# Row factors brought to the partitions by DMA instead of by a selection matmul, in the last attention and the last experts of an eight-layer kernel

## The chip, the cores and the metric

The kernel runs on one core of a Trainium2 chip. A core has five engines, each with its own instruction stream worked off in order: TensorE (PE in the profile, with its weight loads as PEld), VectorE (DVE), ScalarE (ACT), GpSimd (POOL) and SyncE (SP). They hand work to each other through semaphores. Transfers are issued by an engine's instruction stream (here SP, ScalarE or GpSimd) and carried out by 16 DMA engines that all share. An instruction that waits holds up all that stands behind it on its engine. The metric is the device time of one launch in microseconds, on the slowest core; with one core there is no other.

## The reference

Four batches of 512 rows with 128 features each pass through eight layers, attention and feed-forward in turn, each followed by an added residual and a layer norm. Two layers matter here.

The last attention has 16 heads of 64 and clipped relative positions, for keys and for values:

```
sim  = q k^T * scale + q . rel_k_table[idx] * scale
attn = softmax(sim)
out  = attn v + attn . rel_v_table[idx]
y    = out Wo^T + bo
```

The last layer is a mixture of 16 routed experts of width 64 (four of them chosen for each row, out of two of four groups) and a shared expert:

```
weights, idx = gate(x)                       # per row, 4 of 16 experts
combine = sum over the 4 of one_hot(idx) * weights
routed  = einsum(silu(x w1_e) * (x w3_e), w2_e, combine)
shared  = (silu(x w1_s) * (x w3_s)) w2_s
```

Both layers need one number per row and head (1 over the softmax sum) or per row and expert (the combine weight), multiplied on data that lie with heads or experts on the partitions and rows along the free dimension.

## The kernel before

The layers are stages that run one after another; what a stage leaves over at its end runs beside the next one's start. Inside a stage, work is written as generators ("a slot" is one step of all that are live), and a scheduler orders the instructions of each engine from that.

**Third attention (class `A3`).** (In the kernel's naming; it is layer 3 counted from 0.) Work is cut into 32 units of two heads: unit `t` is pair `t % 8` of batch `t // 8`. Eight items (four blocks of 128 queries, two heads) make a unit, so a unit has eight slots. For each item `score` makes two products into a PSUM bank `s` (L1344, L1345), DVE adds a window and takes the row minimum (L1347, L1349), and ScalarE takes the exponential with the row sum into `den` (L1350). Two items later (`la = 2`) `turn` transposes the result `p` four times on PE (L219) and ScalarE copies it to `PT` (L1363); DVE sums the right part (L1368), and every second time SP stores a band of `p` to DRAM (`a3dpw`, L1372). At the end of a unit SP loads the band's diagonals back (`at`, L1376). `tail` then makes 16 value products in one run (L1393, "the value block"), which needs all `PT` of the unit, and later two small products from `at` (L1406, L1407); ScalarE copies the result to `OT` (L1409). `prep` makes the operands of the next unit: a ScalarE cast `H` (L1307), a DVE remainder `L` (L1308) and nine or so copies inside SBUF, nearly all on SP's queue (L1312). `half` makes, once for four units, the values `V` and the window data `bd`.

Four units make a half of a batch. After each half, `fin` (L1414) divides by the softmax sums. It takes the reciprocal `rd`, splits it in a high and a low part `lr` (L1423, L1424), transposes it to 16 rows, which ScalarE copies to `lT` (L1430), and then, for each of the four `OT` of the half, spreads two of these rows over 64 partitions each with a product by a 0/1 matrix `a3sel`, and multiplies:

```
nc.tensor.matmul(ps, w["sel"][:, pr, :], lT, start=True, stop=True)   # L1436
nc.vector.tensor_tensor(OT, OT, ps, ALU.mult)                          # L1437
```

Then the output product follows (L1447), and after the second half the layer norm. `fin` of the half that ends with unit `t - 1` starts in the first slot of unit `t + 1`, that is, one unit after `t - 1` is through its scores, because its last `OT` comes late in unit `t`.

PSUM: `s` has three banks, `t` two, `o` one and `b` two. Bank `b` serves `prep`, `half` and `fin` in turn.

**Last experts (class `F3`).** For each batch, `hidden` makes nine blocks of 128 hidden features (the shared one first, then eight pairs of experts), each from six products into two banks `s`. `gate` computes the combine weights of a batch on DVE and POOL, transposes them and has ScalarE copy them to `cT`. Four positions behind `hidden`, `weigh` spreads two experts' weights over the partitions with the same kind of product (L2287, bank `t`, of which there is one) and multiplies them on (L2288); two positions later `out` makes the products with the second weights (L2297). The gate of batch `c` is started `ahead = 7` positions before the batch's first `hidden`; a batch has nine positions. If the weights are not there when `weigh` needs them, it steps the gate until they are.

DMAs issued by SP and by ScalarE signal on a shared set of eight completion counters, taken in turn; each DMA waits until the one before it on its counter has landed.

Of the kernel before, what the change touches and what calls it, by code (L numbers as in the profile page):

```python
# [16 lines left out]
P = 128  # L17
NB = 4
# [21 lines left out]
class K:  # L40
# [249 lines left out]
    def split_w(self, pool, src, n, name, scales=(), tag=None, raw=("wraw", 1)):  # L290
# [5 lines left out]
        def fill():  # L296
            for s in range(0, n, 512):
# [10 lines left out]
                yield  # L308
        return h, l, fill()

    def mm3(self, out, wh, wl, xh, xl):
# [801 lines left out]
def a3_constants():  # L1113
    c = {}
    ql = np.arange(P)[:, None]
    x = np.arange(512)[None, :]
    c["c_right"] = (x >= ql).astype(np.float32)
    st = np.zeros((32, 2, 2, T), np.float32)
    for bk in range(32):
        st[bk, :, :, 16 * bk + 32:] = 1.0  # L1120
    c["c_step"] = st.reshape(64, 2, T)
    r = np.arange(16)[None, :]
    c["c_d16"] = (r < 16 - ql % 16).astype(np.float32)
    c["c_sel3"] = heads(8)
    return c


class A3:
# [93 lines left out]
    def operands(self):  # L1222
        k, nc, d, pool, w = self.k, self.nc, self.k.d, self.pool, self.w
        w["right"] = pool.tile([P, 512], BF16, name="a3right")
        nc.gpsimd.dma_start(w["right"], d["c_right"])
        w["sel"] = self.more.tile([P, 4, P], F32R, name="a3sel")
        self.lT = k.rows16(self.more, "a3lT")
        nc.gpsimd.dma_start(w["sel"], d["c_sel3"])

# [148 lines left out]
    def tail(self, t):  # L1378
# [33 lines left out]
        yield  # L1412

    def fin(self, b, hf, X):  # L1414

        k, nc, w, pool = self.k, self.nc, self.w, self.pool
        u = k.next()
        den = self.S[b][2]
        wait = k.turn if b == NB - 1 and hf else lambda: ()
        lr = self.more.tile([P, 4, 16], F32R, tag="lr", name=f"lr{u}", bufs=1)  # L1420
        rd = self.more.tile([P, 4, 8], F32, tag="rd", name=f"rd{u}", bufs=2)
        nc.vector.reciprocal(rd, den[:, :, 8 * hf:8 * hf + 8])
        nc.vector.tensor_copy(lr[:, :, 0:8], rd)  # L1423
        nc.vector.tensor_tensor(lr[:, :, 8:16], rd, lr[:, :, 0:8].bitcast(F32), ALU.subtract)  # L1424
        yield from wait()
        ps = k.bank("b")
        for c in range(4):
            k.tr(ps[:16, c * P:(c + 1) * P], lr[:, c, :])
        lT = self.lT
        nc.scalar.copy(lT[:16], ps[:16, :])  # L1430
        yield
        for pr in range(4):
            yield from wait()
            ps = k.bank("b")
            OT = self.S["O", b, 4 * hf + pr]
            nc.tensor.matmul(ps, w["sel"][:, pr, :], lT, start=True, stop=True)  # L1436
            nc.vector.tensor_tensor(OT, OT, ps, ALU.mult)  # L1437
            yield
# [20 lines left out]
    def run(self, Xs):  # L1459
# [5 lines left out]
        for t in range(n + 1):  # L1465
            if t + 1 < n:
                gs.insert(0, self.prep(t + 1))
            if 1 <= t <= n:
                gs.append(self.tail(t - 1))
            if t >= 5 and t % 4 == 1:  # L1470
                b, hf = divmod((t - 5) // 4, 2)
                gs.append(self.fin(b, hf, Xs[b]))
            if t % 4 == 1 and (t + 3) // 4 < 2 * NB:
                gs.append(self.half(*divmod((t + 3) // 4, 2), Xs[(t + 3) // 8]))
            for j in range(8):
                next(main, None)
                k.step(gs)
                if t > n // 2:
# [701 lines left out]
class F3:  # L2180


    nm, span, keep = "f3", None, True
    lag, ahead, steps = 4, 7, 2
    banks = dict(s=4, t=1, o=1, b=2)
# [17 lines left out]
    def gate(self, b, X):  # L2203
# [48 lines left out]
        nc.vector.reciprocal(den, den)  # L2252
        nc.vector.tensor_tensor(cw, cw, den[:, :, None].to_broadcast([P, 4, 16]), ALU.mult)

        c2 = pool.tile([P, 4, 32], F32R, tag="c2", name=f"c2{u}", bufs=2)
# [7 lines left out]
        yield  # L2263
        cT = self.cTs[b % 2]
        nc.scalar.copy(cT[:32], ps[:32, :])
# [16 lines left out]
    def weigh(self, b, j, h):  # L2282
        k, nc, w = self.k, self.nc, self.w
        while b not in self.cT:
            k.step(self.gs)
        cb = k.bank("t")
        nc.tensor.matmul(cb, w["sel"][:, j, :], self.cT[b], start=True, stop=True)  # L2287
# [20 lines left out]
    def run(self, Xs):  # L2308
# [14 lines left out]
        for i in range(9 * NB + self.lag + 2):  # L2323
            b, j = divmod(i, 9)
            j = (j + 8) % 9
            for c in range(1, NB):
                if i == max(9 * c - self.ahead, 0):
                    gs.append(self.gate(c, Xs[c]))
# [79 lines left out]
```

## Time and profile before

| | us |
|---|---|
| median of three runs | 2243.53 (2236.81 to 2244.39) |
| profiled execution | 2239.62, its span 2237.9 |
| third attention | about 1548 to 2105 of the span |
| last experts | about 2105 to 2237 |
| PE busy | 2025.4 (91% of the span) |
| DVE busy | 1664.1 (74%) |
| ACT busy | 1333.5 (60%) |
| POOL busy | 501.9 (22%) |
| mean granted TensorE clock | 0.965 |

The page lists the busy time of each engine first, then the span in 40 slices of about 56 us, in which a digit is the busy share in tenths. A "group" line names a source line, an engine, an operation and its tiles, how often it ran, its busy time and mean, and how long the engine stood idle just before it and for whom. A "wait" line reads: who waited, at which line, for whom, then total time, number and longest. The "chain" is the work that ended last, followed back from the end: it shows what really took the time where several engines are busy at once. Issuing a DMA and waiting count as no busy time; the queue lines (SPq, ACTq) show issues. Matmuls overlap each other, so the mean of a matmul in a group is longer than what it adds to the chain.

### The profile page before, as it was taken

To read this page: it belongs to the slowest core of one execution; us is meant where nothing else is said; L and a number is where in the kernel's file an instruction comes from. 1 tells how busy PE (TensorE), PEld (TensorE's weight loads), DVE (VectorE), ACT (ScalarE), POOL (GpSimd) and SP (SyncE) were. 2 spreads that over 40 slices of the span, in tenths; PEclk is the share of its full clock that TensorE was granted. 3 is DMA by queue.
4 is the path that set the end of the run, shared out by engine and by line. 5 is a ranking of instruction groups with operands and counts; after the bars stand their busy time and mean duration, and the time that the engine had idled before them with its cause. 6 is when DMAs were issued, how large, how long until landed. Compare 5 with 4: busy or idle time off the path is not lost.

```text
span 2237.9 us, 43122 instructions
## 1 busy us (share of the span) xinstructions
PE 2025.4 (91%) x14400; PEld 1477.7 (66%) x14400; DVE 1664.1 (74%) x5592; ACT 1333.5 (60%) x2983; POOL 501.9 (22%) x706
## 2 busy tenths in 40 slices
PE   7999788888888999999999999998999999999897
PEld 4666566676665667676887665786666566666676
DVE  5778689888878677873777785544777877778787
ACT  3566787787734656665333666333777777767632
POOL 3222212111212532433000322531111111111220
PEclk9999999999978999999999999999999999999999
DMA  5321322021433454421021420604888878888400
GB/s 171 106 77 35 109 50 57 6 48 27 116 113 108 130 175 125 127 65 57 15 67 48 116 78 15 219 17 112 214 209 198 211 192 193 199 194 211 99 5 15
DMA packets 264918, 242.10 MB, mean 108 GB/s; under 512 B 106352, under 2 KB 190618, under 8 KB 263866
## 3 DMA queue, kind: packets, MB, share of 16 engines
q1 hardware_dynamic: 259146, 221.33, 37.2%
q0 software_dynamic: 5232, 17.50, 3.3%
q8 instruction: 115, 1.88, 0.3%
q14 instruction: 105, 0.86, 0.1%
q10 hardware_dynamic: 320, 0.52, 0.1%
HBM read 103.82 MB, written 74.32 MB: 80 GB/s over the span
## 4 chain that ended last, share of the span: by engine, by line
PE 59%; DVE 17%; ACT 10%; DMA 7%; issue 4%; POOL 2%; SPq 1%; ACTq 0%; POOLq 0%; DVEq 0%
PE t L219 5%; PE s L2129 4%; PE o L1393 3%; PE o L744 3%; PE s L695 3%; PE t L728 3%; PE o L1032 3%; PE b L313 3%; PE b L219 3%; PE o L2025 3%; DMA a3dpw<-p 2%; PE s L313 2%; PE b L315 2%; PE b L314 2%; PE s L315 2%
## 5 line engine op out<-in xcount | busy, mean ns | idle before, releaser
L985 DVE CUSTOM_DVE_ANT_0 junk<-w,a1mask 128x640 bf16<-128x640 f32 x256 | 203.1, 818 | 67.3 <-PE w L983 65.4
L219 PE MATMUL t<-ident,p 128*128 128x128 f32 x1280 | 201.9, 279 | 23.8 <-ACT p L1350 15.7
L772 ACT ACTIVATE Pt<-t 128x384 f32<-128x384 f32 (+1 forms) x384 | 179.5, 528 | 65.8 <-PE t L728 54.4
L219 PEld LDWEIGHTS t<-ident,p 128*128 128x128 f32 x1280 | 151.7, 142 | 81.0 <-ACT p L1350 39.0
L1363 ACT COPY PT<-t 128x512 f32<-128x512 f32 x256 | 149.9, 596 | 71.9 <-PE t L219 70.9
L1059 ACT ACTIVATE Pt<-t 128x512 f32<-128x512 f32 x256 | 149.1, 597 | 72.7 <-PE t L1058 44.5
L1350 ACT ACTIVATE p<-s,nb 128x512 f32<-128x512 f32 x256 | 178.6, 702 | 12.8 <-DVE nb L1349 8.4
L1349 DVE TENSOR_REDUCE nb<-s 128x1 f32<-128x512 f32 x256 | 175.0, 687 | 2.6
L1368 DVE CUSTOM_DVE_ANT_0 jk<-p,a3right 128x496 bf16<-128x496 f32 (+3 forms) x256 | 125.0, 488 | 29.2 <-ACT p L1350 17.8
L697 DVE CUSTOM_DVE_ANT_0 junk<-s,a0mask 128x128 bf16<-128x128 f32 (+3 forms) x256 | 114.2, 485 | 43.4 <-PE s L695 42.4
L697 DVE CUSTOM_DVE_ANT_0 junk<-s,a2mask 128x128 bf16<-128x128 f32 (+3 forms) x256 | 114.9, 484 | 28.3 <-PE s L695 27.9
L781 POOL TENSOR_SCALAR_AFFINE_SELECT Pt<-Pt 128x512 f32<-128x512 f32 x112 | 69.9, 636 | 249.0 <-ACT Pt L772 248.9
L1344 PE MATMUL s<-a3KT,a3QT 128*128 128x512 f32 x256 | 118.9, 465 | 7.3 <-DMA a3K<-L 4.1
L1347 DVE TENSOR_TENSOR s<-s,W 128x160 f32<-128x160 f32 (+1 forms) x256 | 81.1, 318 | 56.1 <-PE s L1345 55.2
L1393 PE MATMUL o<-PT,V 128*64 128x512 f32 x512 | 116.9, 599 | 0.5 <-ACT PT L1363 0.5
L1707 ACT ACTIVATE p<-sm,nb 128x128 f32<-128x128 f32 x256 | 100.6, 396 | 24.8 <-DVE nb L1705 24.3
L1345 PE MATMUL s<-a3K,a3Q 128*128 128x512 f32 x256 | 102.7, 401 | 0.1
L1705 DVE CUSTOM_DVE_ANT_0 sm<-s,band,rn 128x128 f32<-128x128 f32 x256 | 78.3, 344 | 26.5 <-PE s L1692 19.3
L1056 PE MATMUL t<-a1Q,a1K 128*128 128x512 f32 (+3 forms) x256 | 92.4, 366 | 6.2 <-ACT Pt L1059 3.6
L695 PE MATMUL s<-a0K,a0Q 128*128 128x256 f32 (+2 forms) x256 | 83.6, 387 | 14.0 <-DVE mx L697 6.8
L982 PE MATMUL w<-a1K,a1Q 128*128 128x256 f32 (+2 forms) x192 | 83.8, 437 | 9.3 <-DVE mx L985 8.3
L2012 ACT ACTIVATE sl<-s 128x512 f32<-128x512 f32 x64 | 38.0, 598 | 91.0 <-PE s L315 85.6
(494 smaller groups left out, 5812.7 us busy)
## 6 DMA issues: line engine op xcount, KB each, us to landing
W<-a3dsk SPq DMA_DIRECT2D x32, 640.0 KB
a1Q<-a1iq SPq DMA_DIRECT2D x32, 512.0 KB
a3dpw<-p SPq DMA_DIRECT2D x64, 160.0 KB
a3dpw<-p SPq DMA_DIRECT2D x64, 144.0 KB
a1K<-a1ik SPq DMA_DIRECT2D x64, 128.0 KB
a3Q<-a3dim SPq DMA_DIRECT2D x32, 256.0 KB
a3KT<-H POOLq DMA_DIRECT2D x64, 128.0 KB, 4.4
a3KT<-H SPq DMA_DIRECT2D x64, 128.0 KB
```

Of the source, the lines that this page charges most:

```text
L219: return self.nc.tensor.matmul(out.bitcast(x.dtype), x, i[:n, :n], is_transpose=True, start=start, stop=stop)
L695: self.scored = nc.tensor.matmul(s[:, :nm], self.qof(0, t, i)[:, qc * P:(qc + 1) * P], Ks[:, i, :nm], start=True, stop=True).ins
L697: nc.vector.tensor_tensor_reduce(junk[:, :n], s[:, :n], k.mask[:, 512 - n:512], 1.0, NEG, ALU.add, ALU.max, mx[:, qc, i:i + 1])
L772: ready = nc.scalar.activation(Pt[:, i, z:], s[:, z:], AF.Exp, scale=sc).ins
L985: nc.vector.tensor_tensor_reduce(junk, s.rearrange("p a n -> p (a n)")[:, T - n:T + m], k.mask[:, T - n:T + m], 1.0, NEG, ALU.add, ALU.max ...
L1059: nc.scalar.activation(Pt[:, i, :T], s, AF.Exp, scale=sc)
L1344: nc.tensor.matmul(s, QT[:, e, qs], KT[:, e, :], start=True, stop=False)
L1349: nc.vector.tensor_reduce(nb, s, AX.X, ALU.min)
L1350: nc.scalar.activation(p[:, e, :], s, AF.Exp, bias=nb, scale=-1.0, accum_out=den[:, qc, 2 * un + e:2 * un + e + 1])
L1363: self.copied[t] = nc.scalar.copy(PT[e][:, :, qc * P:qc * P + P], tb.rearrange("p (c n) -> p c n", n=P)).ins
L1368: nc.vector.tensor_tensor_reduce(jk[:, :nn], p[:, e, x0:], w["right"][:, :nn], 1.0, 0.0, ALU.mult, ALU.add, at[:, e, qc, 31:32])
L1393: m = nc.tensor.matmul(o[64 * e:64 * e + 64, :], V[:, kc, h * 64:h * 64 + 64], PT[e][:, kc, :], start=(kc == 0), stop=False)
```

## The change

Both places get their spread rows from DRAM instead of from a product.

In the third attention a new generator `sums` starts one unit earlier than `fin` used to compute these numbers. It transposes the four columns blocks of the reciprocals as they are (f32, without the split), ScalarE copies eight rows, and ScalarE's own queue stores them to a DRAM tile and loads each row back to 64 partitions, two loads for each of four tiles `rb`. The first tile takes the space of a tile that was used in the setup, the third that of another stage's tile, the second and fourth share the two buffers of `rb` with the rows themselves. `fin` now waits three slots and only multiplies, on SBUF data. `a3sel` and its load, `lT` and its memset are gone.

In the last experts the same is done for the third and fourth batch (`b > 1`), on SP's queue: one store of 16 rows, then four loads of four rows to 64 partitions each. Their gates start nine positions ahead instead of seven. The first two batches keep the product.

```diff
+    def rows_out(self, rows, name, eng):
+
+        d = self.dr.tile([rows.shape[0], T], F32, tag=f"rows{rows.shape[0]}", name=name, bufs=2)
+        eng.dma_start(d, rows)
+        return d
+
+    def rows_in(self, dst, d, i, eng):
+
+        n = dst.shape[1] if len(dst.shape) > 2 else 1
+        for e in range(2):
+            ap = [[0, 64], [2 * T, n], [1, T]] if n > 1 else [[0, 64], [1, T]]
+            eng.dma_start(dst[64 * e:64 * e + 64], bass.AP(tensor=d.tensor, offset=d.offset + (i + e) * T, ap=ap))
...
 class A3: operands
-        w["sel"] = self.more.tile([P, 4, P], F32R, name="a3sel")
-        self.lT = k.rows16(self.more, "a3lT")
-        nc.gpsimd.dma_start(w["sel"], d["c_sel3"])
...
+    def sums(self, b, hf):
+
+        k, nc = self.k, self.nc
+        u = k.next()
+        rd = self.more.tile([P, 4, 8], F32, tag="rd", name=f"rd{u}", bufs=2)
+        nc.vector.reciprocal(rd, self.S[b][2][:, :, 8 * hf:8 * hf + 8])
+        yield
+        if b == NB - 1 and hf:
+            yield from k.turn()
+        ps = k.bank("b")
+        for c in range(4):
+            k.tr(ps[:8, c * P:(c + 1) * P], rd[:, c, :])
+        yield
+        lr = self.more.tile([P, T], F32, tag="rb", name=f"lrow{u}", bufs=2)[:8]
+        nc.scalar.copy(lr, ps[:8, :])
+        yield
+        rb = self.S["R", b, hf] = [pool.tile([P, T], F32, tag=tag, name=f"rb{u}{i}", bufs=n) for i, (pool, tag, n) in
+                                   enumerate(((self.early, "a3z", 1), (self.more, "rb", 2), (k.sh, "oT", 1), (self.more, "rb", 2)))]
+        rows = k.rows_out(lr, f"a3rows{u}", nc.scalar)
+        for i in range(4):
+            for _ in range(1 if i % 2 else 2):
+                yield
+            k.rows_in(rb[i], rows, 2 * i, nc.scalar)
+
     def fin(self, b, hf, X):
 
         k, nc, w, pool = self.k, self.nc, self.w, self.pool
         u = k.next()
-        den = self.S[b][2]
         wait = k.turn if b == NB - 1 and hf else lambda: ()
-        lr = self.more.tile([P, 4, 16], F32R, tag="lr", name=f"lr{u}", bufs=1)
-        rd = self.more.tile([P, 4, 8], F32, tag="rd", name=f"rd{u}", bufs=2)
-        nc.vector.reciprocal(rd, den[:, :, 8 * hf:8 * hf + 8])
-        nc.vector.tensor_copy(lr[:, :, 0:8], rd)
-        nc.vector.tensor_tensor(lr[:, :, 8:16], rd, lr[:, :, 0:8].bitcast(F32), ALU.subtract)
-        yield from wait()
-        ps = k.bank("b")
-        for c in range(4):
-            k.tr(ps[:16, c * P:(c + 1) * P], lr[:, c, :])
-        lT = self.lT
-        nc.scalar.copy(lT[:16], ps[:16, :])
-        yield
+        for _ in range(3):
+            yield
         for pr in range(4):
-            yield from wait()
-            ps = k.bank("b")
             OT = self.S["O", b, 4 * hf + pr]
-            nc.tensor.matmul(ps, w["sel"][:, pr, :], lT, start=True, stop=True)
-            nc.vector.tensor_tensor(OT, OT, ps, ALU.mult)
+            nc.vector.tensor_tensor(OT, OT, self.S["R", b, hf][pr], ALU.mult)
             yield
...
 class A3: run
+            if t >= 4 and t % 4 == 0:
+                sums = self.sums(*divmod((t - 4) // 4, 2))
             if t >= 5 and t % 4 == 1:
                 b, hf = divmod((t - 5) // 4, 2)
                 gs.append(self.fin(b, hf, Xs[b]))
...
             for j in range(8):
                 next(main, None)
+                if j == (self.la if t < n else 0) and t >= 4 and t % 4 == 0:
+                    gs.append(sums)
                 k.step(gs)
...
 class F3
-    lag, ahead, steps = 4, 7, 2
+    lag, ahead, steps = 4, 9, 2
...
 class F3: gate
+        if b > 1:
+
+            yield
+            yield from k.turn()
+            ps = k.bank()
+            for c in range(4):
+                k.tr(ps[:16, c * P:(c + 1) * P], cw[:, c, :])
+            yield
+            cr = pool.tile([16, T], F32, tag="cr", name=f"cr{u}", bufs=2)
+            nc.scalar.copy(cr, ps[:16, :])
+            cb = [pool.tile([P, 4, T], F32, tag="cb", name=f"cb{u}{i}", bufs=2) for i in range(2)]
+            rows = k.rows_out(cr, f"f3rows{b}", nc.sync)
+            for i in range(2):
+                k.rows_in(cb[i], rows, 8 * i, nc.sync)
+            self.cT[b] = cb
+            return
...
 class F3: weigh
+        if b > 1:
+            nc.vector.tensor_tensor(h, h, self.cT[b][j // 4][:, j % 4, :], ALU.mult)
+            return
...
 class F3: run
-                if i == max(9 * c - self.ahead, 0):
+                if i == max(9 * c - (self.ahead if c > 1 else 7), 0):
                     gs.append(self.gate(c, Xs[c]))
```

## The prediction

> **What bounds the kernel now.** I read the page first (shares and slices), then the stretches, the groups and the waits of the third attention, and last its time line and its chain.
>
> ```profile
> PE 2025.4 (91%) x14400; PEld 1477.7 (66%) x14400; DVE 1664.1 (74%) x5592; ACT 1333.5 (60%) x2983; POOL 501.9 (22%) x706
> ...
> PE   7999788888888999999999999998999999999897
> ```
>
> One core, TensorE busy nearly throughout. The change touches only 1620 to 2238 us: up to the first half of the third attention the instructions of both builds stand in the same order on every engine.
>
> ```profile
> 1700.00:1800.00 100.00, 93.92 (x537) 62.82 (x536) 78.58 (x231) 71.34 (x170) 13.61 (x23) 1.00 0.85 195
> 1800.00:1900.00 100.00, 92.68 (x507) 62.49 (x506) 77.82 (x229) 73.44 (x172) 13.35 (x23) 0.98 0.84 194
> ...
> 2150.00:2237.00 87.00, 73.58 (x447) 61.48 (x445) 71.22 (x246) 21.92 (x34) 15.42 (x20) 0.98 0.05 13
> ```
>
> The columns are the stretch, its length, busy time of PE, weight load, DVE, ACT and POOL, the clock, and the DMA engines' share. In the attention PE is busy 93%, ACT only 71 to 73%, but the 16 DMA engines 84%. In the experts (last line) PE and DVE are close together and DMA is empty. The next question is where ACT's missing quarter lies.
>
> ```profile
> L1350 ACT ACTIVATE p<-s,nb 128x512 f32<-128x512 f32 x242 | 168.8, 702 | 11.8 <-DVE nb L1349 8.0 <-ACT p L1350 1.1 <-ACT PT L1363 0.7
> ...
> L1436 PE MATMUL b<-a3lT,a3sel 128*128 128x512 f32 x28 | 13.0, 463 | 0.3 <-DVE OT L1437 0.3
> ```
>
> ```profile
> ACT PT L1363 <- PE t L219: 69.1, 67, 4.3
> ACT V L1280 <- PE b L315: 15.4, 14, 4.0
> ```
>
> Over half of ACT's waiting is 69.1 us for transposes, and the time line says when: while PE runs the 16 value products of one unit in a block (3.58 us), ACT runs dry; outside it ACT has little left.
>
> ```profile
> 1776.07 1.12 ACT L1363 COPY PT<-t 128x512 f32<-128x512 f32 x2
> 1777.03 0.75 ACT L1350 ACTIVATE p<-s,nb 128x512 f32<-128x512 f32 x1
> ...
> 1779.41 0.28 ACT L1350 ACTIVATION_READ_ACCUMULATOR p<-s,nb 128x1 f32 x1
> 1781.44 0.58 ACT L1363 COPY PT<-t 128x512 f32<-128x512 f32 x1 [1.75 <-PE t L219]
> 1783.34 0.59 ACT L1363 COPY PT<-t 128x512 f32<-128x512 f32 x1 [1.32 <-PE t L219]
> ```
>
> ```profile
> 1776.90 3.58 PE o L1393 x16
> 1780.49 0.43 PE b L1436
> 1780.91 0.44 PE t L219 x4
> 1781.35 0.23 PE b L1436
> ```
>
> From 1766.2 to 1779.7 ACT has one gap of 0.41 us. The block starts at 1776.90, right after the last PT copies; it needs them. So on the path PE and ACT alternate, and ACT work ahead of a block delays the block. The chain prices a sel product at 0.23 us, not the 463 ns of its group.
>
> **Part 1, third attention: what goes.** Per half of a batch (8 halves; in 7 the new work lies inside the loop): four products of `a3lT` with `a3sel`, 4 x 0.23 = 0.92 us of PE, and four turns of a PSUM bank `b`; on DVE the cast and the subtract of `lr`, 0.18 + 0.18 us. Each half takes some 24 banks `b`; waits of its weight loads and products for DVE's `L` are 13.4 + 9.2 us over the stage, so four banks fewer could give up to 4/24 x 22.6 = 3.8 us in all. POOL loses one load and one memset at the start, on no path.
>
> **What stays.** Four small transposes, now plain f32 (278 ns against 252 in the groups of L219): nothing to 0.1 us. The reciprocal and the ScalarE copy (570 ns) only move a unit earlier. The four multiplications read SBUF instead of PSUM. The nearest row for that form is
>
> ```profile
> L1669 DVE TENSOR_TENSOR kr<-kr,rn 128x512 f32<-128x512 f32 x32 | 21.2, 682 | 0.1
> ```
>
> against 680 ns for L1437: no gain. [...]
>
> **What comes.** Nine DMA issues per half on ScalarE's own queue: one store of 8 rows and eight loads of 64 x 2 KB. The trace has ScalarE issuing 64-partition DMAs only at the stage's start:
>
> ```profile
> 1546.50 0.62 ACTq L1312 DMA_DIRECT2D a3QT<-L  x1
> 1547.16 0.61 ACTq L1312 DMA_DIRECT2D a3Q<-H  x1
> ```
>
> That is 8 x 0.61 + about 0.4 (SP's `at` issue is 0.36) = 5.3 us of ACT per half, and it isn't in the busy sums. An issue may run beside the instruction before it; for the second of a pair nothing is left to hide under. In the changed order of instructions the first pair of loads stands ahead of the last two PT copies of the unit, so ahead of the block; the other three pairs stand after them, mixed with the exponentials, PT copies and `bd` copies of the next unit. Behind each waiting issue all of these queue, and PE waits for them.
> - Store and first pair: 0.4 + 1.2 us where ACT is full. From 0 (wholly beside other work) to 1.6; I take 1.5, since ACT has no gap there.
> - Three pairs: 3.7 us, against ACT's gaps from 1781.44 to 1795.30: 1.32 + 0.40 + 0.28 + 0.36 + 0.29 + 0.31 + 0.32 = 3.28 us.
> - Waits at the issue. The order shows that SP's and ScalarE's DMAs share eight completion counters in turn: each waits for the DMA eight before it. For ScalarE these are SP's `a3Q`, `at` and `a3KT` copies, or its own load of a pair before. The one landing that the trace prices for a 128 KB copy is POOL's a3KT, 4.4 us; its own load of 2.9 us earlier (two issues, an exponential, a copy) would cost 1.5 us. From 0 to a landing for each of three pairs, 13 us; I take 1.5, the nearest pair.
> So after the block 3.7 + 1.5 - 3.3 = 1.9 us, and per half 1.5 + 1.9 = 3.4. As ACT sets the pace there, PE's 0.92 us buys nothing. Seven halves: +24 us. I reduce it to +20, as DVE's short work and the fewer banks give some back.
>
> **DMA and SP.** 64 loads of 128 KB in all, 8 MB on 107. At the boundary of halves the DMA engines are least full (0.69 of 1777 to 1795), so I cost the traffic at nothing; if that room is not there, one landing, 4.4 us, per half. SP's DMAs wait for the shared counters of ScalarE's late loads: 0 to 4.4 us per half, taken as hidden by the same room. The last half lies beside the experts' start, where DVE splits weights: 0 to 4.4 us, taken as 0.
>
> [...]
>
> **Part 2, last experts, batches 3 and 4.**
>
> ```profile
> L2288 DVE TENSOR_TENSOR h<-h,t 128x512 f32<-128x512 f32 x32 | 21.8, 683 | 6.8 <-PE t L2287 6.3
> ```
>
> Sixteen sel products go: 16 x 0.23 = 3.7 us of PE, plus at most half of the 6.3 us that DVE waits for them. The multiplications cost the same. The gate starts two of nine positions earlier, 2 x 29/9 = 6.4 us (29 us is a third of the 87 us stretch). It must cover a store, then two 512 KB loads: f3sel, 512 KB on an empty queue, landed in 3.8 us, so some 2 + 3.8 + 1.9 = 7.7 us. Before, copy to first weighing was 2.1 us (2139.8 to 2141.9), so 8.5 us are there. SP has only output stores besides, and the second pair's wait for the buffers of batch 3 ends long before its use. I take -3 us; from -7 (all waits gone) to +8 (a landing uncovered in both batches).
>
> **Sum.** +20 - 3 = +17 us. The profiled execution took 2239.6 us (span 2237.9 and 1.7 around it), 3.9 under the median of the three runs. 2239.6 + 17 = 2256.6; half of that offset added, as a new median need not share it, gives 2258.5.
>
> **Rivals.** (a) The issues hide: ACT is idle 27% on average, and half of each pair may run beside an ACT instruction. Then PE's gain counts: 8 x 0.92 + 3.8 + 3 = 14 us, 2239.6 - 14 = 2226. Against it: ACT's idle time sits in the blocks, not where the issues stand. This is the case on the other side; it decides if ScalarE's holding time per half stays under the 3.3 us of gaps. (b) Waiting replaces issuing: the counters and the loads land late in 84% full DMA engines, ScalarE stands for one more 4.4 us landing per half: 7 x 4.4 = 31 us more, 2289. For it: SP already waits 53.3 us for `a3dpw` stores between 1600 and 2060. (c) The halves cancel: the first pair hides, 7 x 1.9 - 3 = +10, less 3.8 for banks: +6, 2246. That the change does not do what it says I exclude: the order shows both parts.
>
> **How the numbers follow.** Forecast 0.53 (own range 2250 to 2275), (a) 0.18, (b) 0.13, (c) 0.16. The range reaches to most of (a) and (b): 2229 to 2287. About 0.5%, 11 us, can be told from no change: against 2243.5, faster is below 2232 and slower above 2255. Faster 0.18; same: (c) and the lower edge of the forecast, 0.25; slower 0.57.
>
> **What would show it.** ACTq issues of 0.6 us in pairs, value blocks of the unit after each half starting 3 us later than the PE work before them needs, ACT waits for DMA where before were none; PE idle up by some 20 us between 1620 and 2085. In the experts DVE's wait for `t` halves. Wrong it would be if the ACTq issues overlap ACT's work, if value blocks keep their distance of 16 to 20 us, or if DVE stands at the multiplications for loads that have not landed.

## The result and the profile after

The changed kernel takes 2283.3 us (median of 6; 2277.5 to 2289.6) against 2245.2 us for the kernel before on the same chip (6; 2236.8 to 2247.4): a ratio of 1.0176, 95% interval 1.0158 to 1.0193. The medians lie 38 us apart; by the ratio it is 39 us. The prediction said 15 us more. The time lies in its wide range and the sign is right, but it is beyond the forecast's own 2250 to 2275, and the runs below point to two things for most of the loss that the sum had at nothing.

The page of the changed kernel, busy times and the slices of PE:

```profile
PE 2024.8 (89%) x14352; PEld 1474.5 (65%) x14352; DVE 1662.4 (73%) x5572; ACT 1331.7 (58%) x2981; POOL 501.1 (22%) x704
...
PE   7999788888878999999999998998898889888897
```

PE does the same work less the products that went; its share fell from 91 to 89%, in the third attention. In stretches (columns as before: the stretch, its length, PE, weight load, DVE, ACT, POOL, clock, DMA share, GB/s) for the whole loop of the attention, first the kernel before, then the changed one:

```profile
1560.00:2090.00 530.00, 498.61 (x2790) 334.17 (x2788) 414.88 (x1209) 393.32 (x930) 69.60 (x123) 0.99 0.85 201
```

```profile
1560.00:2090.00 530.00, 471.21 (x2577) 314.42 (x2576) 382.25 (x1119) 369.08 (x871) 66.77 (x115) 0.97 0.85 201
```

PE is idle 27 us longer, ACT is less busy too, and the granted clock is 0.97 for 0.99. The waits of the changed kernel in the same stretch (engine, line, what it waited for: us in total, times, longest):

```profile
ACT p L1359 <- DVE nb L1358: 39.1, 30, 6.0
...
DVE OT L1456 <- DMA rb<-a3rows: 19.7, 13, 2.6
...
ACT p L1359 <- DMA a3Q<-H: 10.6, 4, 3.9
...
ACT dh L1260 <- DMA a3Q<-H: 4.4, 1, 4.4
ACT PT L1372 <- DMA a3QT<-H: 4.1, 1, 4.1
```

ACT's waits for DMA sum to 30.1 us over all its rows there, against 8.3 us before, and the transfers that it stands for are mostly not the new ones: all but 3.5 us are for copies that every unit had already, most of them issued by SP. The first line is a second thing: ACT waits for `nb`, so for scores that are late, up to 6.0 us at a time. Before that wait was

```profile
ACT p L1350 <- DVE nb L1349: 6.9, 17, 1.0
```

One such place in the chain of waits of the changed kernel (start, us, what):

```profile
1983.38 3.65 PE o L1402 x16
1987.04 0.40 PE s L1353
1987.43 6.71 DMA a3Q<-a3dim
...
1994.16 4.13 DMA a3KT<-H
...
1998.38 0.59 ACT H L1316
```

This is the stretch ahead of the value block of unit 23. After the block of unit 22, 11 us in a row belong to copies: `a3Q` and `a3KT`, both on SP's queue (POOL had issued its two `a3KT` of that moment at 1984.67). In these 11 us PE works, with gaps of up to 1.12 us; then comes the cast of H, and the next block starts at 2006.73, 23.3 us after the one before. ScalarE runs dry beside the block of unit 22, until the next scores come (the wait in brackets):

```profile
1988.81 0.69 ACT L1359 ACTIVATE p<-s,nb 128x512 f32<-128x512 f32 x1 [4.43 <-DVE nb L1358]
```

To place the loss, the 32 value blocks (the groups of 16 matmuls `o<-PT,V` in PE's time line) are laid beside those of the kernel before: for each the interval to the block before it, less the same interval in the kernel before. With t the number of the unit, 4k its first in a half, the sums over the halves are:

```
blocks        4k     4k+1   4k+2   4k+3   first to last
changed     +1.4    +17.9  -11.4  +28.3   +36.3
```

So 36 of the 41.6 us between the two spans arise in the attention, and before two kinds of block: that of unit 4k+1 and that of unit 4k+3 (11 us are won back before those of 4k+2). The stretch shown above is of the second kind: unit 23 is a 4k+3. The experiments use this table throughout.

### The profile page after: what moved, and what is told of

It reads as the page before. It is cut to its first block, busy times and chain, and to the rows that moved or that the text cites. A ratio compares the mean times of both kernels' runs of the same rounds, so it can differ in the third digit from the quotient of the medians.

```text
span 2279.5 us, 43084 instructions
## 1 busy us (share of the span) xinstructions
PE 2024.8 (89%) x14352; PEld 1474.5 (65%) x14352; DVE 1662.4 (73%) x5572; ACT 1331.7 (58%) x2981; POOL 501.1 (22%) x704
## 4 chain that ended last, share of the span: by engine, by line
PE 57%; DVE 16%; ACT 11%; DMA 11%; issue 4%; POOL 1%; SPq 1%; ACTq 0%; DVEq 0%; POOLq 0%
PE t L219 4%; PE s L2152 4%; PE o L1402 3%; PE s L708 3%; PE t L741 3%; PE o L757 3%; PE o L1045 3%; PE b L219 3%; PE o L2048 2%; PE b L326 2%; DMA a3dpw<-p 2%; PE s L326 2%; PE s L328 2%; PE b L328 2%; PE s L327 2%
## 5 line engine op out<-in xcount | busy, mean ns | idle before, releaser
L1356 DVE TENSOR_TENSOR s<-s,W 128x144 f32<-128x144 f32 (+1 forms) x256 | 80.6, 318 | 94.3 <-PE s L1354 92.8
L710 DVE CUSTOM_DVE_ANT_0 junk<-s,a2mask 128x128 bf16<-128x128 f32 (+3 forms) x256 | 114.8, 484 | 28.4 <-PE s L708 28.0
L1354 PE MATMUL s<-a3K,a3Q 128*128 128x512 f32 x256 | 107.3, 419 | 0.4 <-DMA a3K<-L 0.4
L1395 POOL CAST a<-at 128x256 fp32r<-128x256 f32 x32 | 13.4, 420 | 371.7 <-DMA at<-a3dpw 309.9
```

The costliest lines, as they stand in the source:

```text
L710: nc.vector.tensor_tensor_reduce(junk[:, :n], s[:, :n], k.mask[:, 512 - n:512], 1.0, NEG, ALU.add, ALU.max, mx[:, qc, i:i + 1])
```

## The experiments

In all of them "us more" is the amount by which the ratio lies over 1, times about 2243 us. Each ratio is against the kernel before on the same chip, and its interval is 3 to 12 us to either side; a difference of two ratios carries the uncertainty of both. Where copies are said to be unused, they are added to the kernel before, whose selection products compute the result as always. Results at a glance; the last four columns are the sums of intervals:

```
run                                     ratio [95%]             4k   4k+1  4k+2  4k+3
e1  experts' part alone                 1.0014 [0.9995, 1.0033]  +4.9  +0.6  +5.3  -1.2
e2  attention part alone                1.0196 [1.0170, 1.0223]  +1.0 +19.7 -11.8 +30.7
e3  before, products two slots later    1.0066 [1.0040, 1.0092]  -8.5  +0.7  -3.2 +29.7
e4  before, unused copies, ScalarE      1.0139 [1.0113, 1.0165]  +4.3 +20.0  -0.3  +2.9
e5  the same, GpSimd                    1.0157 [1.0138, 1.0177]  -5.4 +34.6  -0.4  +0.3
e6  attention part, SP issues           1.0149 [1.0120, 1.0179]  -7.9  +6.2  -2.3 +38.2
e7  attention, slots of before          1.0181 [1.0156, 1.0205] +15.4 +10.6  -0.9  +3.8
e8  the same, GpSimd                    1.0101 [1.0070, 1.0131]  -1.8 +15.7  +1.1  +4.6
e9  before, sums moved, no copies       1.0007 [0.9993, 1.0022]  -5.8  +1.2  +3.5  +2.8
e10 as e4, 16 of 512 numbers            1.0038 [1.0018, 1.0059]  +3.3  -1.5  -0.7  +2.1
e11 change, one load per tile           1.0679 [1.0650, 1.0709]  +4.4 +109.8 -9.4 +28.5
e12 as e7, one load per tile            1.0662 [1.0626, 1.0698] +35.4 +84.6  +0.2  +8.7
e13 as e4, 256 of 512 numbers           1.0063 [1.0041, 1.0086]  +2.9  +5.4  +0.4  +6.4
e14 as e4, loads later (first try)      1.0110 [1.0067, 1.0152]  -7.8 +29.0  -0.8  +7.9
e15 as e4, loads of 128 partitions      1.0142 [1.0088, 1.0197]  +4.0 +22.6  +0.5  +9.4
e16 as e3, output product in one slot   1.0015 [0.9994, 1.0036]  -7.2 +19.7  -9.3  +1.5
e17 as e4, loads two units later        1.0240 [1.0212, 1.0268] +13.1 +10.3  +0.0 +28.4
e18 change, output product in one slot  1.0143 [1.0115, 1.0171]  +2.5 +34.9  -8.3  -5.5
```

The sums are from one profile each, and good to some 2 us; the ratios are from all runs. e16 is a warning for their use: without any DMA added it has +19.7 before blocks 4k+1 and -16.5 before those of 4k+2 and 4k together, so time can move from one kind of block to another, and one column alone doesn't name a cause.

### The two parts apart (e1, e2)

e1 has the diff's lines in class F3 only, e2 those in class A3 only.

> The kernel before with the experts' part of the change alone (rows by DMA for batches 3 and 4, gates started nine positions ahead); the attention as before. By the traces the stretch from the last value block to the end was 134.3 us before and 137.6 us after. If the experts' part owns that, this runs about 3 us slower than before, and DVE shows waits around the gates. If those 3 us only come from the attention's last half, which overlaps the experts' start, this runs 3 us faster, as the prediction had it.

> The kernel before with the attention's part of the change alone. All theories agree that it carries most of the loss: the value blocks drift by 36 us between the first and the last. Expected +34 to +41 us; if the two parts interact it is clearly less.

The experts' part can't be told from no change (+3 us, interval -1 to +7); the loss is in the attention (+44).

### The late products alone (e3)

```diff
 class A3: fin, of the kernel before, ahead of the loop over pr
+        for _ in range(2):
+            yield
```

> The kernel before, with two empty slots ahead of the four selection products, so that the multiplications and the output product come at the same slots as in the changed kernel. No DMA is added, nothing is issued by ScalarE. Theory 'late slots': the output product, which holds one of two banks b for four slots, now falls on the next unit's operand products, the casts H of every fourth unit come late, and this alone costs 20 to 28 us, in the interval before the value block of unit 4k+3. Rival 'issuing' (ScalarE's nine issues per half) and rival 'landings' (loads late, DMA full): within 4 us of before.

Two empty slots, with no DMA added, cost 15 us (interval 9 to 21), less than the 20 to 28 expected, and the loss stands before blocks 4k+3: +29.7 in the one profile, with 11 us won back elsewhere. That is the second of the two places in the table of the changed kernel. The wait for late scores is there as well, in the waits of e3:

```profile
ACT p L1350 <- DVE nb L1349: 33.3, 27, 6.8
```

### The loads alone, by ScalarE and by GpSimd (e4, e5)

```diff
 class A3: fin of the kernel before; its reciprocals, lr, transposes and
 the copy to a3lT become sums(), one unit earlier, and then
+        rows = k.rows_out(self.lT[:8].bitcast(F32), f"a3rows{u}", nc.scalar)
+        for i in range(4):
+            for _ in range(1 if i % 2 else 2):
+                yield
+            rb = ...   # the tiles a3z and oT in turn; nothing reads them
+            k.rows_in(rb, rows, 2 * i, nc.scalar)     # e5: nc.gpsimd, twice
```

> The kernel before, with the reciprocals, transposes and the row copy moved one unit earlier, and with the change's nine DMAs per half issued by ScalarE at the same slots as in the changed kernel; what they load is not used, and the multiplications still take the selection products at their old slots. Theory 'issuing': 24 to 36 us slower, ACT held at the issues. Theory 'landings' in its DMA-traffic form: the same 20 to 30 us, but spread over SP's waits. Theory 'late slots': 4 to 10 us slower (5.3 us of issues per half against 3.3 us of gaps), with no extra in the interval before the block of unit 4k+3.

> As the run with the unused loads, but GpSimd issues the nine DMAs per half instead of ScalarE: the same bytes in the same slots, ScalarE neither issues nor waits, and GpSimd's DMAs do not take the eight counters that SP and ScalarE share. Theory 'ScalarE held' (issues of 0.45 to 0.6 us and 22 us of ACT waits for landings in the run with ScalarE): 0 to +6 us against before. Rival 'traffic' (8 MB more in DMA engines that are 84% busy): at least +15 us.

The products stay in their slots, and the loss before blocks 4k+3 is gone; that before blocks 4k+1 stays. With GpSimd issuing, ScalarE is held by no issue, and it costs the same (+35 for +31 us): this goes against the prediction's main term, that the issues hold ScalarE, as far as copies are concerned that nobody reads. But both runs had also moved the sums, so they needed a control.

### Control, and the bytes (e9, e10, e13)

e9 is e4 without `rows_out` and the loop of loads. e10 and e13 are e4 with shorter rows:

```diff
-            ap = [[0, 64], [2 * T, n], [1, T]] if n > 1 else [[0, 64], [1, T]]
-            eng.dma_start(dst[64 * e:64 * e + 64], ...)
+            ap = [[0, 64], [1, 16]]                   # e13: 256
+            eng.dma_start(dst[64 * e:64 * e + 64, :16], ...)
```

> Kernel before, with only the sums moved: reciprocals, transposes and the copy of the rows stand one unit earlier, as in the two runs with unused copies, but no DMA is added and the selection products stay. It is the control for those two runs (+31 us with ScalarE issuing, +34 us with GpSimd). Theory T, the loads themselves cost the time (their traffic, or what they delay): 0 to +8 us against the kernel before, and intervals before the block of units 4k+1 about as before (0 to +6 us in sum). Rival O, the order alone costs it (the four transposes and the copy now stand in a full place): +20 to +34 us, with +15 us or more before the blocks of units 4k+1.

> As the run with unused copies by ScalarE (+31 us), with the same nine issues per half, the same queue and the same counters, but each load brings only 16 of 512 numbers of each row (64 x 64 bytes in place of 64 x 2 KB); the copies are used by nothing and the result is computed as in the kernel before. Theory T1, the bytes cost: +0 to +12 us over the kernel before, ScalarE waits for DMA below 6 us in all. Rival T2, the issues and counters cost whatever is moved: +24 to +34 us. If the control without any DMA is itself slow, this one is no faster than the control.

> As the run with unused copies by ScalarE (+31 us with 512 numbers per row, +8.5 us with 16), each load now bringing 256 of 512 numbers per row: the same issues, half the bytes. The copies are used by nothing. Theory T1a, the bytes are paid in proportion: 8.5 + half of 22.5, +16 to +23 us. Rival T1b, the stage has room for some traffic and only the rest is paid: +8 to +13 us. Rival T1c, it is the landing time of a descriptor that is no longer small, not its bytes: +26 to +32 us.

The moved order costs nothing that can be told (+1.6 us by the ratio). The same 72 issues and counters with 1/32 of the bytes cost +8.5 us, half of the bytes +14, all of them +31. So most of the cost, 31 - 8.5 = 22.6 us (some 7 us to either side), is in the bytes, and about 7 us (some 6 to either side) in issues and counters. The other part of the evidence is ACT's waits for DMA. The longest rows of 1560 to 2090 us, of e9, of e10 and of e4:

```profile
ACT H L1320 <- DMA a3Q<-H: 3.8, 5, 1.2
...
ACT dh L1264 <- DMA a3Q<-H: 3.5, 2, 2.1
...
ACT dh L1264 <- DMA a3KT<-H: 0.8, 1, 0.8
```

```profile
ACT p L1363 <- DMA a3dpw<-p: 4.4, 4, 2.1
...
ACT p L1363 <- DMA a3Q<-H: 2.4, 2, 1.5
...
ACT dh L1264 <- DMA a3Q<-H: 2.3, 1, 2.3
```

```profile
ACT bd L1283 <- DMA a3KT<-H: 10.8, 2, 5.5
...
ACT p L1363 <- DMA rb<-a3rows: 4.2, 2, 3.2
...
ACT bd L1283 <- DMA rb<-a3rows: 3.8, 1, 3.8
...
ACT p L1363 <- DMA a3Q<-H: 2.9, 1, 2.9
ACT p L1363 <- DMA a3dpw<-p: 2.8, 2, 2.3
```

and of e5, where ScalarE issues none of them:

```profile
ACT p L1363 <- DMA a3dpw<-p: 8.4, 3, 3.4
...
ACT dh L1264 <- DMA a3K<-L: 6.5, 1, 6.5
...
ACT dh L1264 <- DMA a3KT<-H: 5.5, 1, 5.5
```

Summed over all rows of that kind: 8.3 us before, 9.2 in e9, 12.0 in e10, 19.2 in e13, 31.2 in e4, 27.2 in e5. In these runs that follows the time, roughly. What ACT stands for are the copies of before and the stores of `p`; only in e4 are 8.0 us of it for the new loads themselves, of which two in turn take each tile, and e5 loses as much without them. The reading is that the copies of before land later beside 1 MB more per half, and free the tiles that ACT wants to write, or bring what PE needs, later. That step is argued, not shown: the one copy whose landing the traces time, POOL's `a3KT`, has a median (1600 to 2090 us) of 4.4 us before, 5.0 in e4 and 5.5 in e5, but 4.8 in e9 and 4.1 in e13. Whether the cost is in proportion stays open: half of the bytes in proportion would be 20 us, the reading that some room was there gives 8 to 13, and the interval of e13 is 9 to 19.

### The bytes at another moment (e14, e17)

In e14 the first load waits 16 slots more. In e17 the store takes its rows from the OT tile of unit 4k+1, so that no load can stand before unit 4k+2:

```diff
-        rows = k.rows_out(self.lT[:8].bitcast(F32), f"a3rows{u}", nc.scalar)
+        src, at = self.lT[:8].bitcast(F32), divmod(8 * b + 4 * hf + 5, 8)
+        if at[0] < NB:
+            while ("O", *at) not in self.S:
+                yield
+            src = self.S[("O", *at)][:8]
+        rows = k.rows_out(src, f"a3rows{u}", nc.scalar)
```

> As the run with unused copies by ScalarE (+31 us, +20 of them before the blocks of units 4k+1), with the eight loads two units (16 slots) later, in units 4k+2 and 4k+3, the store as there. Same bytes, issues and counters; used by nothing. Theory T1d, the stage has no room for 8 MB wherever they stand: +25 to +35 us, the loss now before the blocks of units 4k+3 and 4k+4. Rival T1e, it is the moment (the start of a half, where its own copies are due): +0 to +14 us.

> Second try at the question of the moment: in the run before it the eight loads moved in ScalarE's order by only two or three exponentials, not by two units, since the order of the queue is planned. Here the store takes its 8 rows from the OT tile of unit 4k+1, so that it and the loads can't stand earlier than unit 4k+2, some 18 exponentials (two units and a quarter) later than in the run with unused copies (+31 us). Same bytes, issues and counters, used by nothing; in the last half they stand as before. Theory T1d, the attention has no room for 8 MB wherever they stand: +20 to +35 us, the loss (+20 us before blocks 4k+1) now before blocks 4k+3 and 4k+4. Rival T1e, the moment costs it (the start of a half): +0 to +13 us.

e14 says nothing on this: the planner moved the loads by two or three exponentials only, and the loss stayed before blocks 4k+1. In e17 they did move by two units, the loss moved with them (+28.4 before 4k+3, +13.1 before 4k), and it grew to 54 us, more than either theory had. So the bytes were free at neither of the two moments tried; the "least full" boundary of the prediction was, if anything, the better one. Part of the 54 us is the experiment's own: ScalarE's loads now come soon after the store they wait for, as

```profile
ACT p L1363 <- DMA a3rows<-OT: 8.8, 3, 3.3
```

shows. How much is not separated.

### Half the issues (e11, e12, e15)

```diff
 rows_in; e11 in the changed kernel, e12 in e7
+        if n == 1:
+            eng.dma_start(dst, bass.AP(tensor=d.tensor, offset=d.offset + i * T, ap=[[T, 2], [0, 64], [1, T]]))
+            return
```

> The whole change, with the 8 loads of 64 partitions per half in the attention made 4 loads of 128 partitions: half the issues, the same bytes. The changed kernel takes some 38 us more than before. Theory T1 (bytes) together with the late slots: +32 to +40 us, nothing gained. [...]

> The attention part alone, with the sums two slots earlier and the multiplications in the slots of the kernel before (the late slots undone), ScalarE issuing, and 4 loads of 128 partitions per half in place of 8 of 64. With 8 loads this order took +39 us, with GpSimd issuing 8 loads +20 us. Theory T1 (bytes): +30 us or more, as with 8 loads. Rival T2 (issues): +10 to +22 us. If both halves of the issues and the late slots were all there is, it would come to the kernel before or below.

e15 is e4 with `ap=[[0, 128], [1, T]]`, one row for all 128 partitions:

> As the run with unused copies by ScalarE (+31 us), with four loads of 128 partitions per half in place of eight of 64: half the issues, the same bytes. Each load takes 128 rows that follow one another in DRAM by zero distance (one row for all partitions), so that the outer dimension of its source counts 128; in the two runs with one load per tile it counted 2, DMA moved some 50 GB/s at a share of 0.13 for 20 us, and the whole took 150 us more. Used by nothing. Theory B, bytes cost and the 150 us came from the outer dimension of 2 (two of 16 engines): +22 to +30 us, landings as with 64 partitions. Rival C, a load over 128 partitions is slow in itself: +90 us or more. Rival I, issues cost after all: +10 to +18 us.

One load per tile (e11) took 152 us more than before, 113 more than the changed kernel; no theory on record had that. DVE's time line in e11 shows why: it waits for each tile in turn (the wait in brackets), 7.5 and 7.7 us apart.

```profile
1739.25 0.69 DVE L1459 TENSOR_TENSOR OT<-OT,rb 128x512 f32<-128x512 f32 x1 [4.62 <-DMA rb<-a3rows]
...
1746.73 0.70 DVE L1459 TENSOR_TENSOR OT<-OT,rb 128x512 f32<-128x512 f32 x1 [5.74 <-DMA rb<-a3rows]
...
1754.44 0.69 DVE L1459 TENSOR_TENSOR OT<-OT,rb 128x512 f32<-128x512 f32 x1 [6.48 <-DMA rb<-a3rows]
```

and the DMA engines of e11 between 1734 and 1755 us (40 slices, busy tenths, then GB/s):

```profile
DMA  4999941111118987111111119259999111111111
GB/s 97 206 272 180 215 109 43 45 50 53 45 50 210 237 192 154 41 50 50 49 47 55 47 55 234 86 144 226 195 297 300 54 47 55 47 48 50 49 49 51
```

While only these loads are left, the digit is 1 (10 to 20%) and some 50 GB/s are moved. That is what 2 of 16 engines (0.125) would give, and the outer dimension of the source counts 2. In e15 it counts 128, the loads again cover 128 partitions, and the time is that of e4 (1.0142 against 1.0139). Nobody reads these loads, so the time alone doesn't say when they land; but SP's queue, which waits for ScalarE's DMAs on the shared counters, stood 88.0 us for such loads in e11 between 1560 and 2110 (17 times), and 2.1 us in e15 (twice). And between 1560 and 2090 us the DMA engines moved 202 GB/s in e15 and 206 in e4, against 177 in e11. So 128 partitions are not slow here; the source's form was. Half the issues brings nothing measurable here: 32 issues fewer in e15, an estimated 32 x 0.46 = 15 us of ScalarE, and no gain, though e15's interval is wide (20 to 44 us).

### The issuing engine, and the products in their old slots (e6, e7, e8)

e6 is e2 with `nc.sync` for `nc.scalar` in `rows_out` and `rows_in`. e7 is e2 with the sums two slots earlier and the products in the slots of before (so it has no experts' part); e8 is e7 with `nc.gpsimd`:

```diff
-                if j == (self.la if t < n else 0) and t >= 4 and t % 4 == 0:
+                if j == 0 and t >= 4 and t % 4 == 0:
 ...
 fin
-        for _ in range(3):
+        for _ in range(1):
```

> The attention's part alone, with the nine DMAs per half on SP's queue instead of ScalarE's. Late slots stay (+15 us in the run of their own). Theory 'ScalarE held': what is left is that, +12 to +20 us, plus what SP's held copies cost; SP feeds the operands of the next unit, so up to +10 more. Rival 'ScalarE is not it': as the attention's part from ScalarE, +44 us.

> The changed kernel, but the reciprocals start two slots earlier and the multiplications wait one slot instead of three, so that multiplications and output product come at the slots of the kernel before. The DMAs stay with ScalarE. If late slots (15 us) and held ScalarE (31 us) add, this takes 11 to 16 us off the changed kernel: +25 to +30 us against before, and the interval before the block of unit 4k+3 is as before. If the loads land too late for the earlier multiplications, DVE waits for them instead and nothing is won.

> The attention's part alone with both causes taken away: two slots earlier as above, and the DMAs issued by GpSimd. If the two causes are all, what is left is the gain that the prediction's rival (a) had priced for the attention: 0.92 us of PE per half and fewer banks b, 7 to 11 us faster than before. If DMA traffic or GpSimd's slower issue holds the loads up, DVE waits at the multiplications and it is within 5 us of before or slower.

None of the three came out as expected: e6 lost 33 us for at most 30, e7 41 for 25 to 30, and e8, which was to win 7 to 11, lost 23. In e7 and e8 the loss before blocks 4k+3 falls to some +4, as in e4. In e6, with the late products, it is there (+38). But the sum doesn't follow: e7 as a whole gained some 3 us on e2, within the uncertainty, and the loss appeared before 4k and 4k+1. Between e7 and e8 only the issuing engine differs (a load took GpSimd 549 ns to issue in e8, at the mean, and ScalarE 462 in the changed kernel, at the median), and that is worth 18 us; between e2 and e6, with SP for ScalarE, it is worth 11 (some 9 to either side of both), and between e4 and e5 it is worth -4. So where the copies are used, ScalarE's issuing may well cost something near the prediction's 20 us; why it does so there and not with copies that nobody reads isn't settled. ACT's waits for DMA don't follow the time here either: 8.1 us in e6, no more than before, and 22.2 in e7.

### Why late products cost (e16, e18)

```diff
 fin, output product; e16 in e3, e18 in the changed kernel
         for c in range(4):
             for pr in range(4):
                 nc.tensor.matmul(y[:, c * P:(c + 1) * P], ...)
-            yield
+            if c == 3:
+                yield
```

> Kernel before with the selection products two slots later (alone +14 us, +30 of them before the blocks of units 4k+3), and with the 16 matmuls of the output product in one slot in place of four, so that its bank is held for one slot. No DMA added; the result is computed in full. In the order of instructions the cast of H for the units 4k+3 then stands one or two exponentials further ahead than with the late products alone (as in the kernel before). Theory L, the late slots cost because the output product holds one of two banks into the next unit's preparation: -8 to +6 us, and no loss before the blocks of units 4k+3. Rival M, the later multiplications themselves cost, by the OT that they finish: +10 to +20 us, with that loss unchanged.

> The whole change (+38 us), with the 16 matmuls of the output product in one slot in place of four; nothing else. With the late products alone this took the loss from +14 us to +3 us. Theory, loads and late slots are two causes that add: +23 to +30 us, and the sum before blocks 4k+3 falls from +28 to below +12 us. Rival, in the whole change the loads' delay alone holds the multiplications back (DVE waits 22 us for them), so that the output product is late however it is issued: +34 to +40 us.

The output product holds one of the two banks `b` over four slots. With the products late, these slots reach into the next unit's `prep`, which needs banks `b` for its projections; in ACT's order of instructions the cast of H of units 4k+3 then stands two or four exponentials before that unit's first, where it was five. With the output product in one slot the late products cost nothing that can be told (1.0015 for 1.0066; in e16 the cast stands five or six ahead), and the wait for late scores is back near its size of before, 6.9 us, in e16 and, for the most part, in e18:

```profile
ACT p L1350 <- DVE nb L1349: 10.2, 20, 0.9
```

```profile
ACT p L1359 <- DVE nb L1358: 15.0, 22, 4.2
```

(39.1 in the changed kernel.) In the whole change the loss before blocks 4k+3 is gone, as expected (+28 to -5.5), but the total fell by less, to 1.0143: 7 us of 39, with an uncertainty as large; neither theory's range held it. The loss before blocks 4k+1 rose (+17.9 to +34.9). That need not be the bytes: the same edit raised it as much in e16 (+19.7, for +0.7 in e3), where no DMA is added. By the totals e18 lies at e4 and e16 together, 31 + 3 = 34 us for 32. So in this pair of runs the two causes can well add; e7, which takes the late slots away by another order, says that they don't. This stays open.

None of the versions is faster than the kernel before.

## Why the prediction was wrong

- **Where the loss sits.** Right in part: "value blocks of the unit after each half starting 3 us later" measured 17.9 / 7 = 2.6 us (of which 1.6 are won back before the next block), "ACT waits for DMA where before were none" rose from 8.3 us, so there were some, to 30.1 us, PE's idle time "up by some 20 us" 27 us. The 28 us before blocks 4k+3 was not in it at all. One of its own signs of being wrong came true: DVE stood 19.7 us at the multiplications for loads that had not landed.
- **"I cost the traffic at nothing"** is the step that failed most. It was read from the DMA share of one stretch, 0.69 at the half boundary, as if room in the mean were room for a copy that something waits for. With copies that nobody reads the bytes cost 22.6 us (e4 against e10), and no less at the other moment (e17). The alternative in the prediction, one landing of 4.4 us per half "if that room is not there", would have been 7 x 4.4 = 31: nearer, and it is the price of rival (b), whose total of 2289 came closest. Rival (b) gave ScalarE's standing at its own issues as the reason; in e5 ScalarE issues nothing, and the loss is the same. So its nearness is in part luck: it had the landings too high, and nothing for the late products.
- **The issues on ScalarE**, the sum's main term with +24 reduced to +20, were too high as far as copies that nobody reads can tell. One load's issue measured 462 ns, not 610:

```profile
L322 ACTq DMA_DIRECT2D rb<-a3rows x64: 452/462/882, 1634.9 to 2150.8; - x64
```

  (min/median/max.) Issues and counters together cost 7 us (e10 against e9), about 1 us per half for the 3.4 predicted: there ACT's gaps hide more than the prediction gave them. With the copies in use, ScalarE's issuing was worth 11 and 18 us (e2 against e6, e7 against e8), so for the changed kernel this term isn't settled.
- **The later products** (`fin` waits three slots) got no price; this is the second step that failed. They cost 15 us alone (e3), through the output product that holds its bank into the next unit (e16). The prediction followed every instruction that was moved, but not what a later OT does to the instructions that were not.
- **The multiplications from SBUF** had no gain by the row (682 against 680 ns). The changed kernel shows

```profile
L1456 DVE TENSOR_TENSOR OT<-OT,rb x32: 669/691/5878, 1641.1 to 2157.4; 128x512 f32<-128x512 f32 x32
```

  against 664/680/689 before: 11 ns more at the median. The row was nearly right. (The maximum is one instruction of the last half, at 2149.03, after a wait for its tile.)
- **The experts**, -3 us, measured +3 with 4 us of uncertainty (e1). DVE's wait for `t` halved as said, from 6.3 us; but PE now waits for DVE's first products. Of the changed kernel, and then of the kernel before, between 2090 us and the end:

```profile
PEld o L2339 <- DVE h L2326: 6.9, 3, 3.1
PE o L2339 <- DVE h L2326: 5.6, 3, 2.6
...
DVE h L2330 <- PE t L2329: 3.3, 3, 1.4
```

```profile
PEld o L2297 <- DVE h L2288: 1.4, 2, 0.7
...
PE o L2297 <- DVE h L2288: 0.6, 2, 0.3
```

  PE and DVE were close together in that stretch, as the prediction said; with work taken from PE alone, the wait is now on PE's side.
- **Rival (a)**, issues hide and 14 us are won, is false. Its first half, that issues hide, is nearly true for copies that nobody reads; it missed the bytes and the late products.

In sum: 1.6 for the order, 7 for issues, 22.6 for bytes and 15 for the late slots make 46; the attention alone measured 44 (e2), the whole change 39. That is near, but no proof: each price was taken alone, in the kernel before, which still has its selection products, and the same sum without the late slots, 31, missed e7 by 10 us.

## What to carry to other kernels

Where the DMA engines are as busy through a stage as here (0.85 between 1560 and 2090 us) and copies lie on its chain of waits, added bytes may have to be paid; here they were, with ScalarE issuing (+31 us in e4) and with GpSimd (+35 in e5), and at both moments tried (+54 in e17). Price them, or measure them with copies that nobody reads, at full size and at a fraction. When a step is put later, look for what it holds meanwhile (here a PSUM bank) and who asks for it next. The shape of an access pattern can cost more than the transfer's size: with an outer dimension of 2 at the source the same bytes took 113 us more than in the changed kernel, and some 50 GB/s were moved while only these loads were left (e11); with 128 the time was that of e4 (e15).

## What was not expected of the hardware

In one place the granted clock fell for a while. After the 11 us of copies in the chain shown above PE's matmuls start 0.43 us apart in place of 0.23, from 2000.80 to 2005.49 us. Stretches of the changed kernel (columns as before; the clock is the third figure from the end):

```profile
1987.00:2000.00 13.00, 9.98 (x54) 7.18 (x53) 10.94 (x31) 9.18 (x22) 1.85 (x4) 0.95 1.10 242
2000.00:2007.00 7.00, 7.00 (x25) 5.31 (x27) 4.03 (x14) 4.44 (x11) 0.31 (x1) 0.60 0.87 228
2007.00:2014.00 7.00, 6.99 (x41) 3.82 (x38) 5.52 (x15) 4.76 (x13) 1.50 (x2) 1.00 0.79 176
```

The clock of 0.60 for 7 us costs 2.8 us there; between 1999 and 2005 it was 0.50. (The DMA share of 1.10 shows that this column is not exact.) Over the 530 us of the attention 0.97 for 0.99 is at most some 10 us of the 36, if all of it lay on the path, with rounding of the same order; the mean was 0.95 in e17 and 0.90 in e11, the runs in which PE stands most (busy 470 and 423 of the 530 us). What sets the clock down isn't shown: ahead of this fall PE's longest idle time was 1.12 us (at 1993.92), with 77% busy over the 13 us.

What stays open: whether the bytes are paid in proportion (e13) and by which wait, why the issuing engine matters in one order and not in another (e4, e5 against e2, e6 and e7, e8), whether the two causes add, and how much of e17's loss is the store that its loads wait for.
